# A four-direction scan block: silu tiles laid out by group, the first gate stores issued later, and the next image's statistics with one weight scaling and seven more small DMAs an image

## The chip, the core and the metric

One core of a Trainium2 chip runs the kernel. It has TensorE (PE, with its weight loads shown apart as PEld), VectorE (DVE), ScalarE (ACT), GpSimd (POOL) and SyncE (SP), which here issues almost every DMA. The metric is the device time of one execution in microseconds; lower is better. Below, "the queue" is SP's queue of DMAs, which is worked off in order: an issue that waits holds up every issue behind it.

## The reference, cut to what matters

For each of 4 images (128 channels, 96 x 96 points) the input is group-normalised (32 groups of 4 channels), read as four sequences (rows forward and backward, columns forward and backward), and each sequence goes through the same block; the four results are fused by a 1x1 convolution and added to the input.

```python
u, gate = split(grouped1x1(groupnorm(x), in_proj_w) + in_proj_b)   # 256 + 256 channels
u = conv_depthwise5(silu(u))
s = ssm_in_w @ u;  a = DMIN + (DMAX - DMIN) * sigmoid(ssm_delta_w @ u + ..)
bb, cc = tanh(ssm_b_w @ u + ..), tanh(ssm_c_w @ u + ..)
h[l] = a[l] * h[l-1] + bb[l] * s[l]                                # the scan
u = u + ssm_out_w @ (cc * h + ssm_d * s)
y = out_proj_w @ grouped1x1(u * sigmoid(gate), mix_w)
```

The normalisation is never applied to x. It is folded into the input projection: the weights are scaled by 1/std of their input channel, and the bias gets the term with the mean subtracted. So each image needs, before its first projection, a scaled weight tile `wn` and a bias tile `bnorm`, made from its mean and variance. The mean of an image's groups is the same for all its points, so this is a small computation, done once for each image.

## The kernel before, in words

The work is cut into 8 phases of 24 iterations, two phases for each image (V for columns, H for rows), 192 iterations `t` in all. An iteration handles one residue of the positions modulo 4 in one of six steps, for a forward and a backward sequence together. The schedule is written out by hand: the order of the statements is the order of each engine's queue, and nothing reorders it. Iterations 0 to 5 run `pair`, the others `pair_on`, which also finishes what iteration t - 6 began.

In an iteration, DVE and ACT make four of the five taps for half the channels, PE makes the other half by banded matmuls (`conv`, and `conv_less` or the separate line `add_lone`), PE projects the inputs of four iterations ahead (`front`, in matmuls of 32 x 32 tiles), ACT turns them into silu, PE makes the projections of the scan (`proj`), DVE scans, POOL multiplies and adds, and PE makes the outputs. The second half of a phase's steps meets the same points as the first half, from the other end, so silus and gates are made in the first half only, stored to DRAM and loaded again later.

What the change touches:

- **The silu tile.** `sil` has, for each of the 128 partitions, 2 sequences x 2 channel halves x 4 groups x 385 values. Its group index is the last but one, so one group is four separate pieces of 1540 bytes in a partition. `keep_silu` stores one group to DRAM, `load_silu` loads one.
- **The first gate stores.** Iterations 0 to 5 make the gates 0, 1 and 2, two iterations for each. At the end of iterations 1, 3 and 5 the finished tile is stored (L935). Gate 2 lies in a borrowed tile and is loaded back at iteration 6.
- **The next image's statistics.** `stats_finish` returns a table of pieces, keyed by (iteration in the phase, place). They run in the first iterations of an H phase, for the next image, so three times in all: phases 1, 3 and 5. `pair_on` calls `piece` at three places: 0 after the recurrence, 1 after the output and gate matmuls, 2 after the gating. The values of the second sequence lie 64 partitions away from those of the first, so `wns` has two versions of the scaled weights, one for each arrangement, and the variance is made in two columns, one for each. `bnorm` has 8 columns, the last four being biases repeated for each quarter of the partitions.
- **The image's data.** `load_front` (L297) loads the inputs of a coming `front`; the loads of a step's first rows (32 partitions x 4 x 385 values, one for each of the tiles `x_in0` and `x_in1`) are issued in the last iteration of the step before, since they overwrite rows that PE has to read first.

Each DMA counts on one of eight semaphores in turn, and an issue waits until the DMA eight places before it has landed; in the rows of the order below these are DMAHW0 to DMAHW7.

Of the kernel before, what the change touches and what calls it, by code (L numbers as in the profile page):

```python
# [42 lines left out]
F32 = mybir.dt.float32  # L43
# [4 lines left out]
P = 128  # L48
# [8 lines left out]
R = 4  # L57
# [11 lines left out]
def conv_preact_kernel(  # L69
# [93 lines left out]
    SC = 384  # L163
    NSC = L // SC
    stats, free = {}, [FRONT[1]]

    def stats_of(b):
        if b not in stats:
# [49 lines left out]
    def stats_finish(b):  # L218

        mv, mean, dev, ex, gm4, var, inv, err, wns, bn = (  # L220
            sp.tile([P] + shape, F32, tag=tag, name=f"{tag}_{b}")
            for tag, shape in (
                ("mv", [2]), ("mean", [1]), ("dev", [1]), ("ex", [1]), ("gm4", [4]), ("var", [2]),
                ("inv", [2]), ("err", [2]), ("wn", [2, P]), ("bnorm", [8]),
            )
        )
        wn, pm = wns[:, 0, :], bank(7)

        def newton():
            nc.gpsimd.tensor_mul(err, inv, inv)  # L230
            nc.gpsimd.tensor_mul(err, err, var)
            nc.gpsimd.tensor_scalar(err, err, -0.5, 1.5, ALU.mult, ALU.add)
            nc.gpsimd.tensor_mul(inv, inv, err)

        def gather():
            nc.vector.bn_aggr(mv, stats[b].rearrange("p c s -> p (c s)"))

        def means():
            product(pm[:, 0:1], gmean, mv[:, 0:1])

        def spreads():
            nc.vector.tensor_copy(mean, pm[:, 0:1])
            nc.gpsimd.tensor_sub(dev, mv[:, 0:1], mean)
            nc.gpsimd.tensor_mul(ex, dev, dev)
            nc.gpsimd.tensor_add(ex, ex, mv[:, 1:2])
            nc.gpsimd.tensor_scalar(gm4, gmask, mean, None, ALU.mult)

        def variances():
            for e in range(2):
                product(pm[:, e : e + 1], gmeans[:, e, :], ex)  # L250

        def guess():
            bits = inv.bitcast(I32)
            nc.vector.tensor_single_scalar(bits, var.bitcast(I32), 1, ALU.logical_shift_right)
            nc.vector.tensor_scalar(bits, bits, -1.0, float(0x5F3759DF), ALU.mult, ALU.add)
            newton()

        def scale_w():
            for e in range(2):
                nc.gpsimd.tensor_scalar(wns[:, e, :], w_in[:, e, :], inv[:, e : e + 1], None, ALU.mult)  # L260

        def biases():
            product(pm[:, 0:4], wn, gm4)
            for g in range(4):
                for q in range(R):
                    mm(pm[:, 4 + g : 5 + g], q, wn[0:32, 32 * g : 32 * g + 32], mean[0:32, :], True, True)

        def finish():
            nc.vector.tensor_sub(bn, b_in, pm[:, 0:8])
# [3 lines left out]
        return {  # L273
            (0, 0): gather,
            (1, 1): means,
            (1, 2): spreads,
            (2, 1): variances,
            (2, 2): lambda: nc.vector.tensor_scalar_add(var, pm[:, 0:2], GN_EPS),
            (3, 0): guess,
            (4, 0): newton,  # L280
            (5, 0): newton,
            (6, 0): scale_w,
            (7, 1): biases,
            (7, 2): finish,
        }

    def half(s):
# [145 lines left out]
    def stats_chunks(t):  # L433
# [5 lines left out]

    sils = {}  # L440

    kept_sil = [
        [dp.tile([P, 2, 2, N + 1], F32, tag=f"sil{e}_{g}", name=f"sil{e}_{g}") for g in range(R)]
        for e in range(2)
# [50 lines left out]

    def load_silu(step, gs):
        if 0 in gs:
            sils[step] = wk.tile([P, 2, 2, 4, N + 1], F32, tag="sil", name=f"sil_{step}")
        for g in gs:
            nc.sync.dma_start(sils[step][:, :, :, g, :], kept_sil[step // NS % 2][g])  # L500

# [101 lines left out]
    def load_last(t):  # L603

        n = NU // 2 - R
        if t == n:
            lasts.append(wk.tile([P, 2, 2, 4, N + 1], F32, tag="sil", name="last_gates"))
# [292 lines left out]
    def pair(t):  # L900
        i = 2 * t
        banks = head_banks(t)
        if t == R:
            load_lone(1)
        if t:
            new_u(i)
            taps(i, range(1, K))
            single = alone(units[i]["p"])
            conv(i, banks, single)
            if single:  # L910
                add_lone(i, banks)
            else:
                conv_less(i, banks, False)
                for s in range(2):
                    nc.vector.tensor_copy(us[i][:, s, 0, :], bank(min(banks) + s)[:, :N])
            first_tap(i + 2)
            front(t + R, FRONT if banks == PROJ else (5, 4, 2, 3))
        recurrence(t)
        stats_chunks(t)
        load_chunks(t + 2)  # L920
        proj(i, banks)
        n, s = divmod(t, 2)
        if s == 0:
            early[0] = tile_of(n) if n < 2 else shared()[:, : 4 * N].rearrange(
                "p (s j n) -> p s j n", s=2, j=2
            )
        for j in range(2):
            gate(2 * n, s, j, 2 + j)
        for j in range(2):
            tanh_one(n, early[0], s, j, 2 + j)  # L930
        load_gate(2 * n + s + UB)
        for g in {0: (0, 1), 1: (2, 3)}.get(t, ()):
            keep_silu(0, g)
        if s:
            nc.sync.dma_start(kept[0][n], early[0])  # L935
# [235 lines left out]
    def start():  # L1171
# [36 lines left out]
        filler(128)  # L1208
        for _ in pieces:
            pass  # L1210
        sils[0] = wk.tile([P, 2, 2, 4, N + 1], F32, tag="sil", name="sil_0")
        banks = ((2, 3), (6, 7), (0, 1), (4, 5)), ((2, 3), (6, 7), (4, 5), (2, 3))

        def burst(j, g):
# [143 lines left out]
```

## Time and profile before

| what | value |
|---|---|
| median of 3 runs | 1743.54 us (1742.93 to 1745.15) |
| profiled execution: its own time | 1740.37 us |
| profiled execution: its span | 1738.6 us |
| PE busy | 1715.3 us, 99% of the span |
| DVE, ACT, POOL busy | 87%, 86%, 84% |
| share of the chain that ended last: PE, DMA | 95%, 2% |
| DMA queue of SP | 64.7% of 16 engines' span |
| granted TensorE clock | 1.0 |

The chain that ended last is followed back from the last instruction. Here it stays on PE nearly everywhere, so what an engine other than PE does matters only where PE is seen waiting for it. Matmuls in float32 show as two records each. A timeline row gives the start, the time from the first start to the last end, the engine, the line, the tiles, how many records were merged, and in brackets the idle time before it with what ended it.

### The profile page before, as it was taken

The numbers are of one execution on the slowest core, as the hardware profiler recorded it, in microseconds if no ns is written. First come the engines' busy times: TensorE is split into PE (matmuls) and PEld (weight loads), VectorE is DVE, ScalarE is ACT, GpSimd is POOL, SyncE is SP. The second block draws the span as 40 slices with busy tenths as digits, with TensorE's granted clock in tenths as the row PEclk, the third lists the DMA queues.
The fourth block names the chain that finished last, engine by engine and source line by source line (L and its number), as shares of the span: only waits on it lengthen the run. The fifth ranks groups of instructions, "written<-read, shape, count | busy, mean of one in ns | idle before, by whom it ended". The sixth has DMA issues, their size and how long they took to land.

```text
span 1738.6 us, 54363 instructions
## 1 busy us (share of the span) xinstructions
PE 1715.3 (99%) x22626; PEld 644.7 (37%) x22626; DVE 1504.6 (87%) x1505; ACT 1494.7 (86%) x2544; POOL 1452.5 (84%) x1496
## 2 busy tenths in 40 slices
PE   7999999999999999999999999999999999999998
PEld 3233333333333433344333443334333343333333
DVE  6899998888889999888888999888888888888897
ACT  4788888889888898888988888888998888888875
POOL 3589889888779988988788988898878889887887
PEclk9999999999999999999999999999999999999999
DMA  7846965368984786337896488433897549743465
GB/s 239 229 157 202 300 194 151 116 214 271 283 280 151 249 272 200 116 124 255 257 309 226 151 298 258 145 120 133 290 287 249 179 140 294 213 135 135 148 224 167
DMA packets 176436, 363.47 MB, mean 209 GB/s; under 512 B 16704, under 2 KB 150848, under 8 KB 176192
## 3 DMA queue, kind: packets, MB, share of 16 engines
q1 hardware_dynamic: 176048, 359.96, 64.7%
q8 instruction: 179, 2.93, 0.7%
q14 instruction: 65, 0.53, 0.1%
q10 hardware_dynamic: 144, 0.04, 0.0%
HBM read 221.41 MB, written 138.53 MB: 207 GB/s over the span
## 4 chain that ended last, share of the span: by engine, by line
PE 95%; DMA 2%; DVE 1%; ACT 1%; issue 0%; SPq 0%; DVEq 0%
PE psum L130 81%; PE psum L564 8%; PE psum L544 5%; DMA x_in<-in_xs 1%; DVE psum L731 1%; DMA acc<-in_xr 0%; DVE u L625 0%; ACT psum L576 0%; DVE u L731 0%; ACT psum L729 0%; SPq L327 0%; PE psum L1188 0%; ACT sil L514 0%; ACT t L777 0%; ACT shared L580 0%
## 5 line engine op out<-in xcount | busy, mean ns | idle before, releaser
L731 DVE SCALAR_TENSOR_TENSOR psum<-sil,small,psum 128x768 f32<-128x768 f32 x576 | 589.1, 1023 | 42.1 <-ACT psum L729 16.6
L130 PE MATMUL psum<-u,w_fin 128*32 128x384 f32 (+1 forms) x6192 | 541.6, 484 | 1.1 <-ACT ys L847 0.5
L130 PE MATMUL psum<-u,main 128*32 128x384 f32 x6144 | 535.1, 489 | 0.5 <-DVE u L678 0.4
L625 DVE SCALAR_TENSOR_TENSOR u<-gate,psum 128x768 f32<-128x768 f32 x376 | 341.8, 950 | 154.7 <-PE psum L564 54.5
L866 POOL TENSOR_TENSOR acc<-ys,acc 128x384 f32<-128x384 f32 x375 | 422.7, 1149 | 13.9 <-ACT ys L847 1.9
L812 POOL TENSOR_TENSOR t<-t,t 64x384 f32<-64x384 f32 (+1 forms) x192 | 277.4, 1445 | 70.8 <-DVE t L806 53.6
L576 ACT COPY psum<-u 128x768 f32<-128x768 f32 x384 | 301.4, 799 | 10.5 <-DVE u L625 4.4
L130 PEld LDWEIGHTS psum<-u,w_fin 128*32 128x32 f32 x6192 | 195.9, 110 | 308.8 <-issue 235.7
L130 PEld LDWEIGHTS psum<-u,main 128*32 128x32 f32 x6144 | 180.0, 109 | 324.5 <-issue 217.4
L130 PE MATMUL psum<-sil,band 128*32 128x384 f32 x3072 | 285.3, 488 | 0.0
L779 POOL TENSOR_SCALAR t<-tm 64x384 f32<-64x384 f32 x184 | 172.5, 937 | 113.4 <-ACT tm L768 101.5
L813 POOL TENSOR_TENSOR t<-t,t 64x384 f32<-64x384 f32 (+1 forms) x192 | 233.9, 1218 | 15.1
L780 POOL TENSOR_TENSOR t<-t,tm 64x384 f32<-64x384 f32 x192 | 213.1, 1110 | 28.4 <-ACT t L771 13.6
L564 PE MATMUL psum<-t,main 32*128 32x384 f32 x1536 | 228.3, 525 | 4.2 <-ACT psum L576 4.2
L729 ACT ACTIVATE psum<-sil,small 128x768 f32<-128x768 f32 x191 | 172.4, 903 | 62.0 <-DVE u L625 60.1
L731 DVE SCALAR_TENSOR_TENSOR u<-sil,small,psum 128x768 f32<-128x768 f32 x192 | 194.9, 1015 | 6.8
L514 ACT ACTIVATE sil<-psum,bnorm 128x385 f32<-128x385 f32 x384 | 191.8, 584 | 7.4 <-PE psum L130 5.2
L544 PE MATMUL psum<-x_in,wn 32*128 32x384 f32 x768 | 161.6, 498 | 0.0
L849 ACT COPY ys<-psum 128x384 f32<-128x384 f32 x288 | 132.4, 478 | 32.9 <-PE psum L130 27.3
L130 PEld LDWEIGHTS psum<-sil,band 128*32 128x32 f32 x3072 | 88.9, 108 | 171.4 <-issue 63.3
L768 ACT ACTIVATE tm<-psum,small 128x384 f32<-128x384 f32 x192 | 110.8, 577 | 16.3 <-PE psum L130 6.2
L564 PEld LDWEIGHTS psum<-t,main 32*128 32x128 f32 x1536 | 94.0, 183 | 73.7 <-issue 42.9
(106 smaller groups left out, 1510.9 us busy)
## 6 DMA issues: line engine op xcount, KB each, us to landing
gate<-kept SPq DMA_DIRECT2D x114, 768.0 KB, 5.7
kept<-gate SPq DMA_DIRECT2D x74, 768.0 KB, 3.6
sil<-sil SPq DMA_DIRECT2D x64, 770.0 KB, 7.8
lone<-edge SPq DMA_DIRECT2D x40, 770.0 KB, 8.5
x_in<-in_xs SPq DMA_DIRECT2D x250, 96.2 KB, 3.3
edge<-sil SPq DMA_DIRECT2D x96, 192.5 KB, 3.9
out<-acc SPq DMA_DIRECT2D x46, 384.0 KB, 6.9
acc<-in_xr SPq DMA_DIRECT2D x39, 384.0 KB, 6.7
```

Of the source, the lines that this page charges most:

```text
L130: nc.tensor.matmul(o[r, : rhs.shape[-1]], lhsT, rhs, start=start, stop=stop, skip_group_check=True)
L514: nc.scalar.activation(sils[step][:, s, j, g, :], bank(bk)[:, : N + 1], AF.Silu, bias=bn[:, 1:2] if j else bn[:, 4 + g : 5 + g],)
L544: nc.tensor.matmul(bank(to)[:, :N], stats[un["b"]][0][r, s, :], x_in[s][r, q, off : off + N], start=True, stop=True)
L564: nc.tensor.matmul(bank(ssm(bi, s) + j)[:, :N], w_so[r, bass.ts(j, P)], z[r, :], start=(bi, s) not in seeded, stop=True, skip_group_check= ...
L576: nc.scalar.copy(psum[:, ssm(bi, s) : ssm(bi, s) + 2, :N], us[bi][:, s])
L625: nc.vector.scalar_tensor_tensor(v, g, 1.0, pz, ALU.add, ALU.mult)
L731: nc.vector.scalar_tensor_tensor(us[i][:, :, 1, :] if k == K - 1 else part, src, w_tap[:, k : k + 1], part, ALU.mult, ALU.add,)
L779: nc.gpsimd.tensor_scalar(*decay(i))
L780: nc.gpsimd.tensor_mul(ta[0:64, p, :], tb[0:64, :], tm[0:64, :])
L812: engine.tensor_mul(ta[0:64, p, r], tb[64:P, r], ta[64:P, p, r])
L813: engine.tensor_add(tb[0:64, r], ta[0:64, p, r], tb[0:64, r])
L866: adder.tensor_add(part, y, part)
```

## The change

Three edits. The silu tile is allocated as 4 groups x 2 x 2 x 385 and addressed through a rearranged view, so a group is one piece of 6160 bytes in each partition; the tile for the last gates has the same layout. The gate stores of iterations 1 and 3 move to iterations 4 and 5; that of gate 2 stays in iteration 5, and comes before that of gate 1. In the statistics of the next image the variance is made in one column and not two; the weights are scaled once, by VectorE and not twice by GpSimd, and the second version is copied from the first by two DMAs inside SBUF (`roll`); the 16 matmuls for the four repeated bias columns go, and the columns are made by storing the first bias column to DRAM (`keep_first`) and loading it back four times, once for each quarter of the partitions (`spread`), each load being 32 partitions x 4 single values.

```diff
-                ("mv", [2]), ("mean", [1]), ("dev", [1]), ("ex", [1]), ("gm4", [4]), ("var", [2]),
-                ("inv", [2]), ("err", [2]), ("wn", [2, P]), ("bnorm", [8]),
+                ("mv", [2]), ("mean", [1]), ("dev", [1]), ("ex", [1]), ("gm4", [4]), ("var", [1]),
+                ("inv", [1]), ("err", [1]), ("wn", [2, P]), ("bnorm", [8]),
...
         def variances():
-            for e in range(2):
-                product(pm[:, e : e + 1], gmeans[:, e, :], ex)
+            product(pm[:, 0:1], gmean, ex)
...
         def scale_w():
+            nc.vector.tensor_scalar_mul(wn, w_in[:, 0, :], inv)
+
+        def roll():
             for e in range(2):
-                nc.gpsimd.tensor_scalar(wns[:, e, :], w_in[:, e, :], inv[:, e : e + 1], None, ALU.mult)
+                nc.sync.dma_start(wns[half(e), 1, :], wns[half(1 - e), 0, :])
 
         def biases():
             product(pm[:, 0:4], wn, gm4)
-            for g in range(4):
-                for q in range(R):
-                    mm(pm[:, 4 + g : 5 + g], q, wn[0:32, 32 * g : 32 * g + 32], mean[0:32, :], True, True)
+
+        def keep_first():
+            nc.sync.dma_start(firsts[b], bn[:, 0:1])
+
+        def spread():
+            for q in range(R):
+                nc.sync.dma_start(bn[32 * q : 32 * q + 32, 4:8], firsts[b].rearrange("(g r) e -> r (g e)", g=4))
...
             (7, 1): biases,
             (7, 2): finish,
+            (8, 2): roll,
+            (9, 2): keep_first,
+            (11, 2): spread,
...
+    def new_sil(of):
+
+        t = wk.tile([P, 4, 2, 2, N + 1], F32, tag="sil", name=f"sil_{of}")
+        return t.rearrange("p g s j n -> p s j g n")
...
-            sils[step] = wk.tile([P, 2, 2, 4, N + 1], F32, tag="sil", name=f"sil_{step}")
+            sils[step] = new_sil(step)
...
         load_gate(2 * n + s + UB)
+        if n == 2 and s:
+            nc.sync.dma_start(keep(n), early[0])
         for g in {0: (0, 1), 1: (2, 3)}.get(t, ()):
             keep_silu(0, g)
-        if s:
-            nc.sync.dma_start(kept[0][n], early[0])
+        if t > 3:
+            nc.sync.dma_start(keep(t - 4), tile_of(t - 4))
```

**SP's queue, iterations 1 to 4.** The first of these rows belong to iteration 1 (the stores of two silu groups `sil_2` and `sil_3`, and the gate store `kept_0`), those with `32x4x385` are the loads of the next step's first rows in iteration 3. Before:

```order
L494 DMA sil_2_204<-sil_291 512x1x385 [waits DMAHW4_49]
L494 DMA sil_3_205<-sil_291 512x1x385 [waits DMAHW5_49]
L935 DMA kept_0_178<-gate_176 128x1536 [waits DMAHW6_49,Activation_49]
L297 DMA x_in_70<-in_xs 32x385 [waits DMAHW7_49,PE_49]
L297 DMA x_in_71<-in_xs 32x385 [waits DMAHW0_49,PE_49]
L429 DMA xs_0_607<-in_xr 128x384 [waits DMAHW1_49]
L315 DMA x_in_70<-in_xs 64x385 [waits DMAHW2_49,PE_49]
L297 DMA x_in_70<-in_xs 32x4x385 [waits DMAHW3_49,PE_49]
L297 DMA x_in_71<-in_xs 32x4x385 [waits DMAHW4_49,PE_49]
```

The same place of the queue in the changed kernel:

```order
L509 DMA sil_2_208<-sil_295 128x1540 [waits DMAHW4_49]
L509 DMA sil_3_209<-sil_295 128x1540 [waits DMAHW5_49]
L307 DMA x_in_70<-in_xs 32x385 [waits DMAHW6_49,PE_49]
L307 DMA x_in_71<-in_xs 32x385 [waits DMAHW7_49,PE_49]
L439 DMA xs_0_610<-in_xr 128x384 [waits DMAHW0_49]
L325 DMA x_in_70<-in_xs 64x385 [waits DMAHW1_49,PE_49]
L307 DMA x_in_70<-in_xs 32x4x385 [waits DMAHW2_49,PE_49]
L307 DMA x_in_71<-in_xs 32x4x385 [waits DMAHW3_49,PE_49]
```

The gate store is gone from between the silu stores and the loads; the second load of first rows waited for the semaphore of `sil_2` (DMAHW4) and now waits for the one before it (DMAHW3, a load of `x_in1`).

**PE, iteration 7 of an H phase, place 1**, where `biases` stands between the output matmuls (L564, now L579) and the scan's projections (`u_1_0_0`). Before:

```order
L564 MATMUL psum<-t_1_0_2_0_2810,main 128x384 x2
L130 MATMUL psum<-gm_1_2577,wn_2581 32x4 [waits Activation_49,Pool_49]
L130 MATMUL psum<-gm_1_2577,wn_2581 32x4 x3
L130 MATMUL psum<-mean_2574,wn_2581 32x1 x16
L130 MATMUL psum<-u_1_0_0_3381,main 32x384 [waits DVE_49]
L130 MATMUL psum<-u_1_0_0_3381,main 32x384 x15
```

And in the changed kernel:

```order
L579 MATMUL psum<-t_1_0_2_0_2814,main 128x384 x2
L130 MATMUL psum<-gm_1_2581,wn_2585 32x4 [waits Activation_49]
L130 MATMUL psum<-gm_1_2581,wn_2585 32x4 x3
L130 MATMUL psum<-u_1_0_0_3380,main 32x384 [waits DVE_49]
L130 MATMUL psum<-u_1_0_0_3380,main 32x384 x15
```

The 16 matmuls on `mean` are gone, and with them the wait for POOL, which no longer makes the weights.

**SP's queue, iterations 9 to 11 of an H phase**, in the changed kernel (`first` is the bias column in DRAM, `kept_5` and `kept_6` gate stores):

```order
L269 DMA first_84<-bnorm_2586 128x1 [waits DVE_49]
L325 DMA x_in_70<-in_xs 64x385 [waits PE_49]
L325 DMA x_in_71<-in_xs 64x385 [waits DMAHW3_49]
L1068 DMA kept_4_198<-gate_180 128x1536 [waits DMAHW4_49,Activation_49]
L325 DMA x_in_70<-in_xs 64x385 [waits DMAHW5_49,PE_49]
L325 DMA x_in_71<-in_xs 64x385 [waits DMAHW6_49]
L1068 DMA kept_5_199<-gate_181 128x1536 [waits DMAHW7_49,Activation_49]
L273 DMA bnorm_2586<-first_84 32x4x1 [waits DMAHW1_49,DMAHW0_49]
L273 DMA bnorm_2586<-first_84 32x4x1
L273 DMA bnorm_2586<-first_84 32x4x1 [waits DMAHW2_49]
L273 DMA bnorm_2586<-first_84 32x4x1 [waits DMAHW3_49]
L325 DMA x_in_70<-in_xs 64x385 [waits DMAHW4_49,PE_49]
```

The four loads stand behind the gate store of iteration 10 and ahead of the two gate-row loads and the gate store of iteration 11.

More of the change, by code (lines that the diff above doesn't have):

```diff
@@ L165, in conv_preact_kernel @@
     stats, free = {}, [FRONT[1]]
+    firsts = [dp.tile([P, 1], F32, tag=f"first{b}", name=f"first{b}") for b in range(B)]
     def stats_of(b):
@@ L258, in scale_w @@
         def scale_w():
+            nc.vector.tensor_scalar_mul(wn, w_in[:, 0, :], inv)
+        def roll():
             for e in range(2):
[L260 removed]
+                nc.sync.dma_start(wns[half(e), 1, :], wns[half(1 - e), 0, :])
         def biases():
             product(pm[:, 0:4], wn, gm4)
[L264 to L266 removed]
+        def keep_first():
[3 more added lines that the diff above has]
+                nc.sync.dma_start(bn[32 * q : 32 * q + 32, 4:8], firsts[b].rearrange("(g r) e -> r (g e)", g=4))
         def finish():
[L269 removed]
+            nc.vector.tensor_sub(bn[:, 0:4], b_in[:, 0:4], pm[:, 0:4])
             nc.gpsimd.tensor_scalar(bn[:, 2:4], bn[:, 2:4], 0.5, None, ALU.mult)
@@ L277, in stats_finish @@
             (2, 1): variances,
-            (2, 2): lambda: nc.vector.tensor_scalar_add(var, pm[:, 0:2], GN_EPS),
+            (2, 2): lambda: nc.vector.tensor_scalar_add(var, pm[:, 0:1], GN_EPS),
             (3, 0): guess,
@@ L497, in load_silu @@
         if 0 in gs:
-            sils[step] = wk.tile([P, 2, 2, 4, N + 1], F32, tag="sil", name=f"sil_{step}")
+            sils[step] = new_sil(step)
         for g in gs:
@@ L606, in load_last @@
         if t == n:
-            lasts.append(wk.tile([P, 2, 2, 4, N + 1], F32, tag="sil", name="last_gates"))
+            lasts.append(new_sil("last"))
         for e in ((0, 1), (), (2,), (3,))[t - n]:
@@ L1210, in start @@
             pass
-        sils[0] = wk.tile([P, 2, 2, 4, N + 1], F32, tag="sil", name="sil_0")
+        sils[0] = new_sil(0)
         banks = ((2, 3), (6, 7), (0, 1), (4, 5)), ((2, 3), (6, 7), (4, 5), (2, 3))
```

## The prediction

> **What bounds the kernel now.** I read the page first: the busy shares and the chain that ended last.
>
> ```profile
> PE 1715.3 (99%) x22626; PEld 644.7 (37%) x22626; DVE 1504.6 (87%) x1505; ACT 1494.7 (86%) x2544; POOL 1452.5 (84%) x1496
> PE 95%; DMA 2%; DVE 1%; ACT 1%; issue 0%; SPq 0%; DVEq 0%
> ```
>
> PE sets the end. A change can help in two ways only: less work on PE, or a place where PE waits. So I looked next for waits, with the chain cut to the first iterations (start, length, what):
>
> ```profile
> 53.93 7.71 DMA x_in<-in_xs
> ```
>
> and at the same place in PE's timeline, with the next iteration for comparison:
>
> ```profile
> 61.78 1.78 PE L130 MATMUL psum<-x_in,wn 32*32 32x385 f32 x32 [1.62 <-DMA x_in<-in_xs]
> 63.48 0.85 PE L130 MATMUL psum<-u,main 128*32 128x384 f32 x8
> ...
> 69.28 1.04 PE L130 MATMUL psum<-x_in,wn 32*32 32x385 f32 x32
> 70.25 2.14 PE L130 MATMUL psum<-u,main 128*32 128x384 f32 x24
> ```
>
> The input projection of iteration 4 starts 1.6 us late, waiting for a DMA of x_in, and then takes 1.70 us (61.78 to 63.48) where iteration 5 takes 0.97. The whole loss is best read from an instruction that every iteration has once, the tanh at L768, in iterations 3, 4 and 5:
>
> ```profile
> 56.56 0.58 ACT L768 ACTIVATE tm<-psum,small 128x384 f32<-128x384 f32 x1 [0.62 <-issue]
> ...
> 65.75 0.58 ACT L768 ACTIVATE tm<-psum,small 128x384 f32<-128x384 f32 x1 [1.06 <-issue]
> ...
> 72.51 0.58 ACT L768 ACTIVATE tm<-psum,small 128x384 f32<-128x384 f32 x1 [0.31 <-issue]
> ```
>
> Iteration 4 takes 9.19 us, iteration 5, with the same matmuls, 6.76: 2.43 us are lost to the late x_in.
>
> **The gate stores and the silu layout.** What is ahead of that load? SP's queue, the DMA shares of those stretches (the two numbers at each row's end are the DMA engines' share and GB/s) and the time to landing of two transfers, by issue window:
>
> ```profile
> 47.44 1.32 SPq L935 DMA_DIRECT2D kept<-gate  x1
> ...
> 53.93 5.92 SPq L297 DMA_DIRECT2D x_in<-in_xs  x4
> ...
> 52.00:56.00 4.00, 3.82 (x72) 1.31 (x68) 2.06 (x4) 3.91 (x8) 2.41 (x3) 1.00 1.09 228
> 56.00:60.00 4.00, 4.00 (x52) 1.09 (x44) 3.03 (x3) 3.38 (x6) 2.70 (x3) 1.00 0.98 293
> ...
> 66.00:68.00 2.00, 2.00 (x20) 0.71 (x20) 1.25 (x2) 1.94 (x5) 1.51 (x2) 1.00 1.07 387
> ...
> kept<-gate SPq DMA_DIRECT2D x1, 768.0 KB, 12.0
> ...
> x_in<-in_xs SPq DMA_DIRECT2D x2, 192.5 KB, 6.8
> ...
> x_in<-in_xs SPq DMA_DIRECT2D x32, 192.5 KB, 4.8
> ```
>
> The DMA engines are full from 52 to 60 us. The gate store issued at 47.44 lands 12.0 us later, so at about 59.4: it is being written just while the wanted x_in loads stand in line. They take 6.8 us, where loads of that size take 4.8 in the whole run. The change takes this store out. It is 768 KB, 786 thousand bytes, and at the 387 GB/s of a stretch with the DMA engines full it is worth 2.0 us of the line, just the difference of 6.8 and 4.8. So the first load lands at 53.93 + 7.71 - 2.0 = 59.6, before PE asks for it at 61.78 - 1.62 = 60.16, and the second need only be there half a projection later. Its issue is also freed: SP spends time before these loads waiting for older DMAs to land (us in all, times, longest, from 36 to 70 us),
>
> ```profile
> SPq L297 <- DMA sil<-sil: 3.7, 3, 1.7
> ...
> SPq L297 <- DMA kept<-gate: 1.3, 1, 1.3
> ```
>
> and in the new order the second load waits for a small load in place of a silu store, while the 1.3 us on the gate store go. Bounds: 2.43 us if the wait vanishes, 0 if the line stays as long as it is. The silu stores become pieces of 6160 bytes; no row has a silu group in that form, and the nearest, the gates, which are of that size and in one piece, land in 3.6 us in the whole run:
>
> ```profile
> kept<-gate SPq DMA_DIRECT2D x74, 768.0 KB, 3.6
> ```
>
> I book nothing for it: at best it shortens the same wait, whose 2.43 us are the bound already, and a loss would need more bytes or more pieces, which there are not. After the start no engine of the chain waits for a silu load, so the layout is worth 0 there.
>
> What is late next? In iteration 5 DVE has little room:
>
> ```profile
> 69.51 1.02 DVE L915 COPY u<-psum 128x384 f32<-128x384 f32 x2 [2.23 <-PE psum L130]
> ...
> 77.70 1.01 DVE L678 SCALAR_TENSOR_TENSOR u<-lone,small,psum 128x768 f32<-128x768 f32 x1 [0.64 <-PE psum L130]
> ```
>
> It was idle 2.23 us before L915, which PE's next projection waits for; of 2.43 us earlier PE work it gives back 0.2. Hence 2.43 - 0.2 = **2.2 us**. The moved stores land where there is room. One more store, of 2.0 us, goes into 72 to 80, in which the DMA share is
>
> ```profile
> 72.00:76.00 4.00, 3.85 (x52) 0.93 (x43) 3.90 (x5) 3.63 (x8) 3.31 (x4) 1.00 0.26 79
> 76.00:80.00 4.00, 2.73 (x32) 0.92 (x32) 3.09 (x6) 3.22 (x6) 3.86 (x4) 1.00 0.50 201
> ```
>
> so 4 x 0.74 + 4 x 0.50 = 5 us are free there; the store of gate 0 comes in iteration 4 in place of the one that iteration 3 issued. The gate tiles they read are written again several iterations later, so nobody waits; without that room the load of gate 2 would be late, whose user comes two iterations after it.
>
> **The statistics, three times.** On PE, 16 matmuls (32 records) on `mean` and 4 of the 8 (8 of 16 records) on `ex` go:
>
> ```profile
> 255.33 0.31 PE L130 MATMUL psum<-ex,gmean 128*32 128x1 f32 x16
> 255.48 0.83 PE L130 MATMUL psum<-u,main 128*32 128x384 f32 x8
> ...
> 299.61 0.24 PE L130 MATMUL psum<-gm,wn 128*32 128x4 f32 x8
> 299.79 0.43 PE L130 MATMUL psum<-mean,wn 32*32 32x1 f32 x32
> 300.14 0.85 PE L130 MATMUL psum<-u,main 128*32 128x384 f32 x8
> ```
>
> Start to start: 0.35 us for the first kind, half of 0.15 for the second, together 0.42 us an image, 1.3 for three. Whole iterations say a little more: the one with the biases, by its tanh, against the same place of a phase without statistics,
>
> ```profile
> 293.30 0.58 ACT L768 ACTIVATE tm<-psum,small 128x384 f32<-128x384 f32 x1 [0.15 <-PE psum L130]
> ...
> 302.36 0.58 ACT L768 ACTIVATE tm<-psum,small 128x384 f32<-128x384 f32 x1 [0.60 <-PE psum L130]
> ...
> 505.01 0.58 ACT L768 ACTIVATE tm<-psum,small 128x384 f32<-128x384 f32 x1
> ...
> 513.52 0.58 ACT L768 ACTIVATE tm<-psum,small 128x384 f32<-128x384 f32 x1 [0.15 <-PE psum L130]
> ```
>
> 9.06 against 8.51: 0.55 for 40 records, of which 8 remain. With 0.08 for those and 0.07 saved on `ex` that is 0.54 an image, 1.6 for three. I take the middle, **1.4 us**.
>
> The Trainium skill (TensorE: Matmul & The Clock Gate, section "Wait — 56ns, not 53.3ns?") says that matmuls never start closer than about 25 ns, however small. By that the 20 matmuls, two records each, would give 20 x 2 x 25 ns = 1.0 us an image, and the sum would be 5.2 us. The row above disagrees: 32 records in 0.35 us are 11 ns each. I leave that rule 1 chance in 50, within the case that more comes out.
>
> The scaling on DVE is one instruction, at the 284 ns of the same operation at the start; POOL loses two of 604:
>
> ```profile
> L260 POOL TENSOR_SCALAR wn<-main,inv 128x128 f32<-128x128 f32 x6 | 3.6, 604 | 0.3
> ...
> L205 DVE TENSOR_SCALAR wn<-main,inv 128x128 f32<-128x128 f32 x2 | 0.5, 284 | 0.0
> ...
> 291.26 0.95 DVE L625 SCALAR_TENSOR_TENSOR u<-gate,psum 128x768 f32<-128x768 f32 x1 [1.45 <-ACT ys L849]
> ```
>
> It comes just ahead of that L625, where DVE idles 1.45 us, so it costs 0 (0.9 us for three if that idle time were gone). Its input is made by POOL an iteration earlier. POOL's 1.2 us an image end no PE wait: 0. The DMAs: `roll` is read nine iterations later, `spread` nine too, and SP has room at `spread`'s place, iterations 10 and 11 of phase 1:
>
> ```profile
> 329.01 0.33 SPq L1051 DMA_DIRECT2D kept<-gate  x1
> 335.04 1.12 SPq L315 DMA_DIRECT2D x_in<-in_xs  x2
> ```
>
> 5.7 us lie between these issues, and the four loads go there: 0, if they take less. No row has loads of single values; the bounds are 0 and the rival below.
>
> **Sum.** 2.2 + 1.4 = 3.6 us. The profiled execution took 1740.37 us, so 1736.8 for the like; the median of the runs shown is 3.2 us above it, and 1743.54 - 3.6 = 1739.9. About 0.2%, or 3.5 us, is what a measurement of this kernel can tell from no change, so the sum stands just beyond that edge.
>
> **Rivals.**
>
> *The wait at 61.78 stays or moves.* The line is full from other stores too, and the two silu stores still stand before x_in. Against it: the 2.0 us fit the excess in landing. Then only PE's 1.4 us are left, or with half the wait 2.5: 1741 to 1742.
>
> *More comes out.* Both upper bounds are reached, 2.43 + 1.6 = 4.0 us, and with the engines shifted against each other the longest wait of PE for ACT, which also lies in the start, goes too:
>
> ```profile
> PE psum L564 <- ACT psum L576: 4.2, 6, 1.3
> ```
>
> That would be 5.3 us, 1738.2. Against it: nothing in the change touches what ACT does there.
>
> *`spread` clogs the queue (the slower side).* Its four loads are 128 single values each, and behind them come a gate store and the next loads. The Trainium skill (DMA: Bandwidth & Descriptors, "Specifications") asks for at least 512 bytes a piece, with a read-modify-write below, and speaks against these. It decides from the point where the four hold SP for longer than its 5.7 us gap and the time until the gate tile is written again, two iterations of 8.5 us less the store's 3.6: 5.7 + 13.4 = 19 us. If each took 6.8 us, one after the other, that is 27 us, 8 late, three times 8 = 24 us: 1743.5 + 24 - 3.6 = 1764. If they overlap, nothing; between the two, with 2.5 us late an image, it is 1743.5 + 7.5 - 3.6 = 1747.4.
>
> *It doesn't do what it says.* DVE or ACT, at 87 and 86%, could hold iteration 5 or 7 just as long, so that the PE time comes back as idle time: 1743.5.
>
> **Numbers.** The forecast has 0.62: 1739.9, of which 0.43 falls beyond the edge and 0.19 within. The wait stays: 0.15, within. More: 0.08, faster. The queue clogs: 0.10, slower. Nothing: 0.05, within. Faster 0.51, same 0.39, slower 0.10. The range is 1737.7 to 1743.3: from both upper bounds (1739.5) down by 1.8, nearly the spread of 2.2 us between the runs shown, and up to almost nothing gained.
>
> **What would show it.** Right: the projection of iteration 4 without a DMA wait and its tanh 6.8 us after that of iteration 3; 8 records of `gm,wn` followed at once by `u,main`; iteration 7 of an H phase at 8.6 us. Wrong: a new PE wait between 60 and 85 us, DVE without idle time ahead of L625 in iteration 6, SP waits behind `spread`, or ACT waiting for a gate store to land.

## The result: about 0.2% faster, with the profile after

| | before | changed |
|---|---|---|
| median of 22 runs each | 1743.50 us (1738.73 to 1749.80) | 1738.99 us (1737.81 to 1746.54) |
| ratio, 95% interval | | 0.9977 (0.9968 to 0.9987) |
| repeated later on one chip, 28 and 12 runs | 1740.48 us | 1737.98 us, 0.9988 (0.9978 to 0.9998) |
| span of the profiled execution | 1738.6 us | 1737.0 us |

In part of the executions of most of these kernels the granted clock is 0.995 to 0.998 of full, and they take about 3 to 8 us longer, so beside the medians I give the difference of the medians of those runs alone that show 0.999 or 1.000 ("at full clock"): for the repetition it is 1737.9 - 1740.0 = -2.1 us. The first comparison has the larger difference with longer runs of the kernel before (their clock is not on record); in the three later comparisons that kernel has 1739.9 to 1740.0 us at full clock.

The page of the changed kernel, busy shares and the chain that ended last:

```profile
PE 1715.6 (99%) x22506; PEld 642.7 (37%) x22506; DVE 1507.8 (87%) x1508; ACT 1494.7 (86%) x2544; POOL 1445.1 (83%) x1490
PE 93%; DMA 2%; DVE 2%; ACT 1%; POOL 1%; issue 1%; SPq 0%; DVEq 0%; POOLq 0%
```

PE has 120 records less (22626 - 22506 = 3 x 40, as counted), yet is busy no shorter. So somewhere PE's records became longer, and the chain leaves PE a little more often.

**The start.** PE's input projection of iteration 4, and the tanh (now L783) of iterations 3, 4 and 5, in the timeline of the changed kernel:

```profile
60.40 1.12 PE L130 MATMUL psum<-x_in,wn 32*32 32x385 f32 x32
```

```profile
56.87 0.58 ACT L783 ACTIVATE tm<-psum,small 128x384 f32<-128x384 f32 x1 [0.62 <-issue]
63.71 0.58 ACT L783 ACTIVATE tm<-psum,small 128x384 f32<-128x384 f32 x1 [0.39 <-issue]
70.45 0.58 ACT L783 ACTIVATE tm<-psum,small 128x384 f32<-128x384 f32 x1
```

The bracket with the DMA is gone, and iteration 4 takes 6.84 us (before 9.19), iteration 5 6.74 (before 6.76). The load that was late lands sooner; these are the DMAs issued from 40 to 60 us of the changed kernel (KB each, median us to landing), with the DMA engines' share and GB/s at each window's end:

```profile
sil<-sil SPq DMA_DIRECT2D x4, 770.0 KB, 6.3
x_in<-in_xs SPq DMA_DIRECT2D x2, 192.5 KB, 4.1
```

```profile
52.00:56.00 4.00, 3.81 (x68) 1.30 (x72) 2.33 (x3) 3.98 (x8) 2.71 (x3) 1.00 0.44 95
56.00:60.00 4.00, 4.00 (x56) 1.21 (x48) 3.06 (x3) 3.31 (x7) 2.39 (x3) 1.00 0.78 196
```

The x_in loads take 4.1 us in place of 6.8, and the engines, full from 52 to 60 us before, now have room there.

**The statistics.** PE in iteration 7 of phase 1, and the tanh on both sides of it:

```profile
297.98 0.25 PE L130 MATMUL psum<-gm,wn 128*32 128x4 f32 x8
298.06 2.77 PE L130 MATMUL psum<-u,main 128*32 128x384 f32 x32
```

```profile
291.67 0.58 ACT L783 ACTIVATE tm<-psum,small 128x384 f32<-128x384 f32 x1
300.25 0.58 ACT L783 ACTIVATE tm<-psum,small 128x384 f32<-128x384 f32 x1 [0.21 <-PE psum L130]
```

The projection follows the 8 records of `gm,wn` at once. The iteration takes 8.58 us where it took 9.06.

**Where time came back.** Lengths of iterations, from one start of the tanh to the next (worked out from the timelines):

| iteration | before | changed | changed, second profile |
|---|---|---|---|
| 4, phase 0 | 9.19 | 6.84 | 6.84 |
| 6 and 7, phase 0 | 9.41 + 8.52 | 10.09 + 8.34 | 9.41 + 8.52 |
| 2, phases 1, 3, 5 | 8.65 | 8.58 | 8.58 |
| 7, phases 1, 3, 5 | 9.05 | 8.58 | 8.58 |
| 9 and 10, phase 3 | 9.12 + 8.32 | 9.12 + **10.47** | **10.47** + 8.40 |

The last row is a new stall, of 2.14 us in the first profile and 1.42 in the second. ACT and PE's chain around it, in the first profile (timeline of ACT, then the chain: start, length, what):

```profile
740.98 0.57 ACT L783 ACTIVATE tm<-psum,small 128x384 f32<-128x384 f32 x1
743.94 0.47 ACT L786 COPY t<-psum 64x384 f32<-64x384 f32 x1 [2.39 <-PE psum L130]
```

```profile
738.85 5.07 PE psum L130 x48
...
743.94 0.47 ACT t L786
...
746.91 0.91 PE psum L559 x2
```

ACT's copy waits 2.39 us for a result of PE; then PE in turn waits for ACT, and the chain makes a detour of 3 us over ACT. Was PE itself held? Its weight loads show the beat (the bracket is the idle time before, "issue" a wait for nothing the profile shows):

```profile
740.76 0.13 PEld L130 LDWEIGHTS psum<-u,main 128*32 128x32 f32 x4 [0.19 <-issue]
...
742.71 0.38 PEld L130 LDWEIGHTS psum<-u,w_fin 128*32 128x32 f32 x4 [0.53 <-issue]
...
743.84 0.46 PEld L130 LDWEIGHTS psum<-u,w_fin 128*32 128x32 f32 x9 [0.46 <-issue]
```

Four loads every 0.32 us (0.13 busy, 0.19 idle) is the regular beat; behind 742.2 us it is broken, and the idle time in these rows is put down to no engine and no DMA. ACT, though, had been idle since its tanh ended at 741.55, before the beat broke; experiment 3 comes back to that. What else happens there? The DMA view of the changed kernel from 733 to 743 us (GB/s in 40 slices of 0.25 us; q8 fetches instructions; landing times at the rows' ends):

```profile
GB/s 393 393 393 393 393 393 393 3 0 0 0 0 66 0 0 0 0 0 0 0 0 0 0 0 0 0 0 0 55 99 31 6 0 0 0 0 6 0 25 86
q8 instruction: 1, 0.02, 2.1%
kept<-gate SPq DMA_DIRECT2D x1, 768.0 KB, 5.9
x_in<-in_xs SPq DMA_DIRECT2D x2, 96.2 KB, 5.7
```

One instruction fetch, begun at 736 us (the 66 in the row of GB/s), lasts 2.1% of 16 engines x 10 us = 3.4 us. The x_in loads take 5.7 us for 96 KB, with stretches in which the engines move nothing though packets are under way. Just ahead, at 732.39, SP issued `keep_first`. Of the small transfers in the whole run,

```profile
wn<-wn SPq DMA_DIRECT2D x6, 32.0 KB, 4.5
bnorm<-first SPq DMA_DIRECT2D x12, 0.5 KB, 2.7
first<-bnorm SPq DMA_DIRECT2D x3, 0.5 KB, 10.3
```

the store of one bias column, half a kilobyte in 128 pieces of 4 bytes, is the slowest by far. That was the theory for the experiments: both gains are there in full, and `keep_first` gives part of them back. How it does so was a guess at this point, that PE lacks its instructions while a fetch is slow.

### The profile page after: what moved, and what is told of

It reads as the page before. It is cut to its first block, busy times and chain, and to the rows that moved or that the text cites. A ratio compares the mean times of both kernels' runs of the same rounds, so it can differ in the third digit from the quotient of the medians.

```text
span 1737.0 us, 54149 instructions
## 1 busy us (share of the span) xinstructions
PE 1715.6 (99%) x22506; PEld 642.7 (37%) x22506; DVE 1507.8 (87%) x1508; ACT 1494.7 (86%) x2544; POOL 1445.1 (83%) x1490
## 4 chain that ended last, share of the span: by engine, by line
PE 93%; DMA 2%; DVE 2%; ACT 1%; POOL 1%; issue 1%; SPq 0%; DVEq 0%; POOLq 0%
PE psum L130 79%; PE psum L579 8%; PE psum L559 6%; DMA x_in<-in_xs 1%; DVE psum L746 1%; DMA out<-acc 1%; DVE u L640 0%; DMA acc<-in_xr 0%; ACT psum L744 0%; DMA kept<-gate 0%; ACT psum L591 0%; DVE u L746 0%; POOL acc L881 0%; POOL t L827 0%; POOL t L828 0%
## 5 line engine op out<-in xcount | busy, mean ns | idle before, releaser
L881 POOL TENSOR_TENSOR acc<-ys,acc 128x384 f32<-128x384 f32 x375 | 410.1, 1115 | 13.2 <-ACT ys L862 1.9
L827 POOL TENSOR_TENSOR t<-t,t 64x384 f32<-64x384 f32 (+1 forms) x192 | 288.0, 1500 | 72.6 <-DVE t L821 50.4
L828 POOL TENSOR_TENSOR t<-t,t 64x384 f32<-64x384 f32 (+1 forms) x192 | 233.8, 1218 | 15.1
L579 PE MATMUL psum<-t,main 32*128 32x384 f32 x1536 | 228.0, 526 | 3.1 <-ACT psum L591 3.0
L783 ACT ACTIVATE tm<-psum,small 128x384 f32<-128x384 f32 x192 | 110.9, 578 | 13.9 <-PE psum L130 2.4
L595 ACT ACTIVATE gate<-psum,bnorm 128x384 f32<-128x384 f32 x152 | 87.9, 581 | 38.7 <-PE psum L559 21.7
```

The lines of the kernel that those rows point to most:

```text
L579: nc.tensor.matmul(bank(ssm(bi, s) + j)[:, :N], w_so[r, bass.ts(j, P)], z[r, :], start=(bi, s) not in seeded, stop=True, skip_group_check= ...
L827: engine.tensor_mul(ta[0:64, p, r], tb[64:P, r], ta[64:P, p, r])
L828: engine.tensor_add(tb[0:64, r], ta[0:64, p, r], tb[0:64, r])
L881: adder.tensor_add(part, y, part)
```

## The experiments

Lengths of iterations are read from the tanh in every run, as above.

**1. The start: stores alone, layout alone, both.** The kernel before, with the later gate stores only:

```diff
+        if n == 2 and s:
+            nc.sync.dma_start(keep(n), early[0])
...
-        if s:
-            nc.sync.dma_start(kept[0][n], early[0])
+        if t > 3:
+            nc.sync.dma_start(keep(t - 4), tile_of(t - 4))
```

> The kernel before with the later gate stores alone. Theory (the gate store stood in the line ahead of x_in): iteration 4, by the tanh after proj, takes about 6.8 us instead of 9.19, and the kernel gains 2 to 2.4 us (ratio about 0.9987). Rival (the pieces of the silu stores are what fills the line): iteration 4 keeps at least 1 us of its 2.4 us of delay, and the gain is under 1.4 us. The iterations with statistics stay at 8.65 (iteration 2 of an H phase) and 9.05 (iteration 7).

Measured: 1738.30 us, ratio 0.9986 (0.9976 to 0.9997), at full clock -1.9 us; iteration 4 takes 6.84 us, all others are as before. With the gate store out of the line the wait is gone, and nothing is given back later.

The kernel before, with the silu layout only:

```diff
-            sils[step] = wk.tile([P, 2, 2, 4, N + 1], F32, tag="sil", name=f"sil_{step}")
+            sils[step] = new_sil(step)
```

> The kernel before with the silu tile laid out by group alone; the gate stores stay in iterations 1, 3 and 5. Theory: the gate store is still in the line, so iteration 4 takes 8.2 to 9.2 us (at most 1 us gained, by larger pieces at a higher rate). Rival (the silu pieces fill the line): iteration 4 takes under 7.8 us, and the gain is 1.4 us or more. If both rivals hold in part, the gains of this run and of the one with the stores alone sum to more than 2.4 us, since the same wait can only go once.

Measured: 1739.01 us, ratio 0.9993 (0.9983 to 1.0003); iteration 4 takes 6.91 us, not between 8.2 and 9.2. But this profile (span 1743.6, clock 0.996) has a lower granted clock ahead of iteration 4, which may have given the DMA queue more time, so the miss settled nothing, and the kernel was run again:

> The kernel before with the silu layout alone, once more, since its first profile had a lower granted clock ahead of iteration 4. Theory as predicted (the layout is worth little by itself): iteration 4 of the start between 8.3 and 9.2 us where the clock is full, time within 1.2 us of the kernel before. Rival (the silu stores in pieces of 6160 bytes leave the DMA queue as much earlier as taking the gate store out does): iteration 4 at 6.9 us at full clock, 1.5 to 2.4 us faster than before.

Measured: 1738.64 us, ratio 0.9988 (0.9978 to 0.9998), at full clock -1.4 us; the profile has clock 1.0 and a span of 1735.8 us. The tanh of iterations 3 and 4 there:

```profile
56.30 0.58 ACT L773 ACTIVATE tm<-psum,small 128x384 f32<-128x384 f32 x1 [0.62 <-issue]
63.14 0.58 ACT L773 ACTIVATE tm<-psum,small 128x384 f32<-128x384 f32 x1 [0.39 <-issue]
```

6.84 us: the rival was right, the layout alone takes the wait away, with the gate store still in front. The same DMA rows and windows as above, for this kernel:

```profile
sil<-sil SPq DMA_DIRECT2D x3, 770.0 KB, 7.4
kept<-gate SPq DMA_DIRECT2D x1, 768.0 KB, 8.6
x_in<-in_xs SPq DMA_DIRECT2D x2, 192.5 KB, 4.1
```

```profile
52.00:56.00 4.00, 3.82 (x68) 1.30 (x64) 2.24 (x3) 3.68 (x7) 2.24 (x2) 1.00 0.78 243
```

And the silu groups of the same stretch in the kernel before:

```profile
sil<-sil SPq DMA_DIRECT2D x4, 770.0 KB, 10.1
```

They land in 7.4 us where they took 10.1, the gate store in 8.6 in place of 12.0, and the engines' share is 0.78 where it was 1.09. The counts of the whole run, of the kernel before and then of this one, show what differs:

```profile
DMA packets 176436, 363.47 MB, mean 209 GB/s; under 512 B 16704, under 2 KB 150848, under 8 KB 176192
q1 hardware_dynamic: 176048, 359.96, 64.7%
```

```profile
DMA packets 151860, 363.47 MB, mean 209 GB/s; under 512 B 16704, under 2 KB 118080, under 8 KB 151616
q1 hardware_dynamic: 151472, 359.96, 62.1%
```

The same bytes go in 24576 packets less and in 2.6% of the span less of all engines' time: 45 us of 16 engines, spread over the silu traffic.

Both together, without the statistics:

> The kernel before with the later gate stores and the silu layout, statistics as before. Theory: iteration 4 takes 6.8 us, and the gain is that of the stores alone to within 0.3 us, 2.1 to 2.5 us (ratio about 0.9987), so the layout adds nothing to the time. Rival: the layout is worth more than 0.5 us on top of the stores, in the start or in the phases after it.

Measured: 1738.36 us, ratio 0.9986 (0.9975 to 0.9998), at full clock -1.7 us, iteration 4 at 6.84. The two edits take the same wait away, so either is enough and the second adds nothing.

**2. The statistics alone, and with the old bias matmuls.** The changed kernel with the old layout and the old stores:

```diff
-        t = wk.tile([P, 4, 2, 2, N + 1], F32, tag="sil", name=f"sil_{of}")
-        return t.rearrange("p g s j n -> p s j g n")
+        return wk.tile([P, 2, 2, 4, N + 1], F32, tag="sil", name=f"sil_{of}")
...
-        if t > 3:
-            nc.sync.dma_start(keep(t - 4), tile_of(t - 4))
+        if s:
+            nc.sync.dma_start(kept[0][n], early[0])
```

> The kernel before with the statistics edits alone (one scaling on VectorE, roll, keep_first, spread, 16 + 4 matmuls fewer an image). Theory: iterations 2 and 7 of phases 1, 3 and 5 go from 8.65 to 8.58 and from 9.05 to 8.58, 0.54 us an image, 1.6 us in all (ratio about 0.9991); iteration 4 of the start stays at 9.2. Rival (the four loads of single values clog the queue): iterations 11 to 14 of phases 1, 3 and 5 grow by 0.5 us or more each time, and the gain is gone.

Measured: 1742.41 us, ratio 1.0007 (0.9995 to 1.0019). At full clock, over five runs only, it is -1.0 us. Iterations 2 and 7 of the three H phases take 8.58 and 8.58 us, so PE gains its 1.6 us; iteration 10 of phase 3 takes 9.37, which is 1.04 lost, in the very place of the changed kernel. Iterations 11 to 14 did not grow, so the rival was wrong, though part of the gain went by another way. Iteration 4 of the start is 8.33 us here, not the 9.2 expected, with the old order and the old layout: what the late load costs differs from run to run.

The changed kernel with the 16 bias matmuls back, and without `keep_first` and `spread`:

```diff
+            for g in range(4):
+                for q in range(R):
+                    mm(pm[:, 4 + g : 5 + g], q, wn[0:32, 32 * g : 32 * g + 32], mean[0:32, :], True, True)
...
-            nc.vector.tensor_sub(bn[:, 0:4], b_in[:, 0:4], pm[:, 0:4])
+            nc.vector.tensor_sub(bn, b_in, pm[:, 0:8])
...
-            (9, 2): keep_first,
-            (11, 2): spread,
```

> The changed kernel with the repeated bias columns made by the 16 matmuls again, without keep_first and spread; scaling on VectorE, roll and the single variance column stay. Theory: iteration 7 of an H phase is 0.46 us longer again (9.05), 1.4 us in three, and iteration 10 of phase 3 is 8.33, 1 to 2.1 us shorter: the two nearly cancel, so within 1 us of the changed kernel. Rival (the single-value DMAs are free): 1.4 us slower than the changed kernel.

Measured: 1738.99 us, ratio 0.9996 (0.9987 to 1.0005), at full clock -1.3 us. Iteration 7 is back at 9.05, iteration 2 stays at 8.58, and no iteration of phase 3 is long: without the store and its four loads there is no stall. Its time is no better than that of the start's edits alone (-1.4 to -1.9), so the cheaper scaling and variance by themselves, 0.07 us an image, can't be told from nothing.

**3. The store in pieces of 512 bytes.** The changed kernel, with `wn` and `bnorm` in one tile `wb`, so that `keep_first` can store 128 neighbouring columns of which the bias is one; 128 times the bytes, the same 128 pieces (the four loads of `spread` still fetch single values, from that column):

```diff
-    firsts = [dp.tile([P, 1], F32, tag=f"first{b}", name=f"first{b}") for b in range(B)]
+    firsts = [dp.tile([P, P], F32, tag=f"first{b}", name=f"first{b}") for b in range(B)]
...
-            nc.sync.dma_start(firsts[b], bn[:, 0:1])
+            nc.sync.dma_start(firsts[b], wb[:, P + 4 : 2 * P + 4])
```

> The changed kernel, but the bias column goes to DRAM in pieces of 512 bytes (128 values a partition, of which one is the bias) and not of 4 bytes; the four loads still fetch single values. Theory (the 128 single-value writes hold up DRAM for some 10 us, and an instruction fetch that falls into it starves PE in iteration 10 of phase 3): the store lands in about 3 us instead of 10.3, no x_in packet after it takes over 2 us, iteration 10 of phase 3 goes from 10.47 back to 8.33 us, and the kernel is 1 to 3 us faster than the changed one (1736 to 1738 us). Rival (it is a chance event of that run, or the place of the instructions): iteration 10 of phase 3 stays above 9 us or falls without the landing changing.

Measured: 1735.91 us (1735.12 to 1737.41), ratio 0.9974 (0.9964 to 0.9985), at full clock -3.9 us, with no long iteration in phase 3 (8.33). This version beats both kernels. Against the changed kernel on one chip:

> The changed kernel once more, beside the version with 512-byte stores on the same chip, with nothing left out. Theory (the single-value store of the bias column is a lottery: whenever its 10 us meet an instruction fetch of PE at a bad moment, PE stands still for up to 2 us, three chances an execution): faster than before by 2 to 4 us; the store again 10 us to landing, at least one instruction fetch of over 2 us beside the three stores, and iteration 10 of phase 1, 3 or 5 longer than 8.4 us in none or one of the three, not surely phase 3 again. Rival (the stall in phase 3 belongs to the place and not to chance): iteration 10 of phase 3 again at 10.4 us, the other two at 8.33. Second rival (the stall was an accident that has nothing to do with the store): none of the three long, no fetch over 2 us there, and a time like that of the 512-byte version.

> The changed kernel with the bias column stored as 512-byte pieces, beside the changed kernel itself on one chip; nothing is left out. Theory: 1 to 2 us faster than the changed kernel, 3.5 to 5 us faster than the kernel before; no fetch of over 2.2 us beside the three stores, iterations 10 of phases 1, 3 and 5 at 8.33. Rival (what separates them is chance of the execution): the two within 0.5 us of one another.

Measured: the changed kernel 1737.98 us (ratio 0.9988, 0.9978 to 0.9998), the 512-byte version 1736.69 us (0.9975, 0.9966 to 0.9984): 1.3 us apart (1.2 at full clock), and its slowest run of ten, 1737.24, is below the fastest of twelve of the changed kernel, 1737.31. The theory held in the size (3.3 us against the kernel before at full clock is just short of 3.5), but not in the picture of a lottery: in the three profiles with the 4-byte store (three such stores an execution) the stall came in phase 3 each time and never in phase 1 or 5, at the tanh of iteration 9 or at the copy right behind it. So the first rival is right in this, as far as three profiles can tell: it belongs to the place. The DMA view of the 512-byte version from 733 to 743 us:

```profile
GB/s 418 492 393 393 266 236 6 0 0 0 0 0 0 0 0 66 0 0 0 0 0 0 0 0 0 0 62 222 111 68 253 74 0 344 418 418 393 393 393 393
q8 instruction: 1, 0.02, 0.7%
kept<-gate SPq DMA_DIRECT2D x1, 768.0 KB, 3.2
x_in<-in_xs SPq DMA_DIRECT2D x2, 96.2 KB, 2.5
```

The fetch takes a third of the time, the gate store and the x_in loads about half. Does the slow fetch hold PE, then? The second profile of the changed kernel says no. These are PE's projections there, ACT's tanh, which waits for their first half, and PE's next weight loads:

```profile
743.35 2.79 PE L130 MATMUL psum<-u,main 128*32 128x384 f32 x32
746.89 0.58 ACT L783 ACTIVATE tm<-psum,small 128x384 f32<-128x384 f32 x1 [1.26 <-PE psum L130]
747.53 0.94 PEld L130 LDWEIGHTS psum<-u,w_fin 128*32 128x32 f32 x16 [0.60 <-ACT tm L783]
```

and the same place with the 512-byte store:

```profile
738.24 2.79 PE L130 MATMUL psum<-u,main 128*32 128x384 f32 x32
740.43 0.58 ACT L787 ACTIVATE tm<-psum,small 128x384 f32<-128x384 f32 x1
741.10 0.47 ACT L790 COPY t<-psum 64x384 f32<-64x384 f32 x1
```

By its records PE keeps its beat in both (2.79 us). Yet the tanh starts 2.19 us after the projections begin with the 512-byte store, and 3.54 us after with the 4-byte store, and only then does PE wait, for ACT. With the statistics alone it is the same: the copy waits 1.29 us for PE behind projections of 2.79 us. So what comes first in the stall is that PE's result reaches ACT late, not that PE is short of instructions. It reaches ACT 11.6, 10.0 and 10.5 us after the issue of `keep_first` in the three profiles, about when such a store lands. And the store itself, in the whole run:

```profile
first<-wn SPq DMA_DIRECT2D x3, 64.0 KB, 3.4
```

128 times the bytes land in 3.4 us in place of 10.3. The Trainium skill (DMA: Bandwidth & Descriptors, section "Specifications") asks for at least 512 bytes a transfer and says that below this the DMA does a read-modify-write; the two landing times agree with it, though no row here shows the read itself.

**4. A dose.** The kernel before with 24 needless stores, one in each of iterations 8 to 15 of phases 1, 3 and 5, first of one value in each partition, then of 512 bytes:

```diff
+    spare = [dp.tile([P, 1], F32, tag=f"spare{k}", name=f"spare{k}") for k in range(8)]
...
+            **{
+                (8 + k, 2): lambda k=k: nc.sync.dma_start(spare[k], stats[b - 1][1][:, 0:1])
+                for k in range(8)
+            },
```

```diff
-    spare = [dp.tile([P, 1], F32, tag=f"spare{k}", name=f"spare{k}") for k in range(8)]
+    spare = [dp.tile([P, P], F32, tag=f"spare{k}", name=f"spare{k}") for k in range(8)]
...
-                (8 + k, 2): lambda k=k: nc.sync.dma_start(spare[k], stats[b - 1][1][:, 0:1])
+                (8 + k, 2): lambda k=k: nc.sync.dma_start(spare[k], stats[b - 1][0][:, 0, :])
```

> The kernel before, with one more store of 128 single values to DRAM in each of iterations 8 to 15 of phases 1, 3 and 5 (24 in all). Theory: each holds up DRAM for some 10 us, instruction fetches of 2 us and more become frequent, and iterations 9 to 16 of these phases grow at several places, by 3 to 15 us in all (1743 to 1755 us). Rival (no effect of such stores): iterations unchanged within 0.1 us, time as before.

> The control to the run with 24 single-value stores: the same 24 stores, of 512 bytes a partition each. Theory: no slow fetches, iterations as in the kernel before to within 0.1 us, time as before. Rival (the number of DMAs or the turn of the eight semaphores is what costs): the same growth as with single values.

Measured: 1742.35 us, ratio 1.0014 (1.0003 to 1.0025), at full clock +2.0 us, against 1739.92 us, 0.9998 (0.9989 to 1.0007), at full clock -0.2 us. The first theory asked for 3 to 15 us, so it was wrong in the size, and its rival (no effect) in kind; the theory of the control held behind the start. Their landing times, in the same order:

```profile
spare<-bnorm SPq DMA_DIRECT2D x24, 0.5 KB, 9.9
```

```profile
spare<-wn SPq DMA_DIRECT2D x24, 64.0 KB, 3.1
```

The width of the pieces makes the difference, not one more DMA in the queue. But the dose isn't in proportion: 24 stores cost 2.0 us, the changed kernel's three cost 1.3. Most of them cost nothing; in this profile iterations 10, 15 and 16 of phase 1 are longer, by 0.68, 0.20 and 0.06 us, 0.9 in all, and none of phase 3. Iteration 10 of phase 1 shows the same late result, 10.1 us after the issue of a store at 311.50:

```profile
317.93 2.79 PE L130 MATMUL psum<-u,main 128*32 128x384 f32 x32
321.62 0.47 ACT L776 COPY t<-psum 64x384 f32<-64x384 f32 x1 [0.93 <-PE psum L130]
```

No slow fetch stands beside it (0.5% of an 11 us window, 0.9 us), and a fetch of over 3 us passed without a stall (at 731.9 us). After the start, a wait of 0.9 us or more of the tanh or of this copy for PE shows in these four profiles with single-value stores, and in none of the nine others.

## Why the prediction was right, and which step failed

The direction and the time were right: 1739.9 us forecast, 1738.99 measured, within the range. That the time is met to 0.9 us is in part luck: the forecast takes 3.6 us off a median, and the medians differ by 4.5 us in the first comparison and by 2.5 in the repetition. At full clock the change is worth 2.1 us and not 3.6.

**"2.2 us" for the start: right, a little small in this profile, large for the mean.** Iterations 4 and 5 gained 2.35 + 0.02 us; the 0.2 us that DVE was to give back did not come. But the profiled execution of before was a dear one: with the old order at full clock iteration 4 took 9.19, 8.33 and 8.48 us in three kernels (before, statistics alone, 4-byte dose; 7.95 in the 512-byte dose, at 0.998), on average 1.8 us above 6.84, and the stores alone gained 1.9 us.

**"I book nothing for it" (the layout): right in the sum, wrong in the reason.** Either edit is enough. That fewer, longer pieces free the DMA engines was left out: the prediction counted bytes, and at the same bytes the layout moved the landing from 10.1 to 7.4 us.

**"The moved stores land where there is room": right.** No wait for them is seen. Iteration 6 grew by 0.68 us in the first profile, at a lower clock (the last section).

**"1.4 us" for the statistics: the upper bound was the true one.** 0.07 us in iteration 2 and 0.47 in iteration 7, three times, is 1.6. Whole iterations were the better measure, since they hold the gaps that rows of instructions leave out.

**"The DMAs: ... 0, if they take less": the step that failed.** The loads of `spread` were weighed, with the rival that they clog the queue. They land in 2.7 us and clog nothing. `keep_first`, 128 pieces of 4 bytes written to DRAM, was not costed at all, although the sentence on pieces under 512 bytes stood beside it. It does not hold SP's queue either; it lands late, and while it is under way an instruction fetch and the reads of x_in take two to three times as long, and in phase 3 PE's result reaches ACT late, for which PE then waits. Price: 2.14, 1.42 and 1.04 us in three profiles, 1.3 us in the time. Without it the two terms come out as summed: 3.3 to 3.9 us for the 512-byte version against 3.6.

**The sum of the spans.** Start -2.4, statistics -1.6, stall +2.1, lower clock in iterations 6 and 7 +0.5; iteration 1 of phase 3, which was 0.2 longer in the one profile before, -0.2; iterations 9 and 10 of phase 6 +0.2; the stretch to the first tanh +0.3, and that behind the last one -0.5: together -1.6 us, which is 1737.0 - 1738.6.

**The rivals.** The wait did not stay; no more came out than the two terms; DVE and ACT did not swallow PE's gain; the queue did not clog. The slower side did exist, by the other end of the same detour through DRAM.

**What stays open.** That the store's narrow pieces cause the stall is shown (4 against 512 bytes, twice, and the version without the store). One thing else moves with the width: the tile in DRAM is 128 times as large, and what lies behind it may be displaced. The version without the store keeps the small tile and has no stall, which speaks against that. By what way the store delays PE's result is not shown. The ends of PE's matmuls are modelled in the profile, so they may have been later than it says, or the word of them was; want of instructions, the theory of the expectations, fits neither the regular beat in two of the three profiles nor the dose, and in phase 1 of the changed kernel a fetch of 2.2% of a 7 us window (2.5 us) stalled nobody. Nor is it shown why phase 3 alone is hit.

## What to carry to other kernels

Cost every DMA that a change adds by the size of its pieces, the stores to DRAM above all: here 128 writes of 4 bytes landed in 10.3 us, 128 writes of 512 bytes in 3.4, and widening them was worth 1.3 us with no instruction saved. Where an engine's idle time has no releaser, look in a second profile for who waited first. Where a load is late behind a full DMA line, count packets as well as bytes, and test the edits one by one, since two that remove the same wait don't add. When PE's count of records falls and its busy time does not, look for the iteration that became longer before believing the sum.

## What the runs showed that I had not expected

**Other transfers take longer beside the small stores, an instruction fetch among them**: the fetch 3.4 us in place of about 1.1, a gate store 5.9 in place of 3.2, x_in loads 5.7 in place of 2.5. For single values loaded into SBUF nothing of the kind is seen: `spread` landed in 2.7 us, and iterations 11 to 14 are no longer.

**The clock in iteration 6.** The windows of the changed kernel from 74 to 78 us (the third number from the end is PE's granted clock):

```profile
74.00:75.00 1.00, 1.00 (x12) 0.37 (x12) 0.96 (x2) 1.00 (x3) 0.92 (x2) 0.57 0.99 399
75.00:76.00 1.00, 1.00 (x12) 0.21 (x4) 0.05 (x1) 0.97 (x3) 1.00 (x2) 0.50 1.05 424
76.00:77.00 1.00, 0.97 (x12) 0.24 (x8) 0.14 (x1) 1.00 (x2) 0.94 (x2) 0.50 1.03 418
77.00:78.00 1.00, 1.00 (x9) 0.31 (x9) 1.00 (x2) 0.19 (x1) 1.00 (x1) 0.73 0.81 332
```

The clock lost is 0.43 + 0.50 + 0.50 + 0.27 = 1.70 us at half speed, so about 3.4 us of it, amid busy PE. The Trainium skill (TensorE: Matmul & The Clock Gate, section "What's actually happening") has a window of 3413 ns and a half clock after an idle one; the length agrees, but PE was busy here. It came in the start with both edits (iteration 6 at 10.08 us) as well, but not in the second profile of the changed kernel nor in the three others with both edits of the start, and what sets it off, the moved stores or not, stays open.

**The end.** From the last tanh to the span's end it is 30.0 to 30.1 us in the five profiles with `keep_first` and `spread`, and 30.5 to 30.7 in the eight without. No experiment was made on it.
